# Dealing the third pass's on-chip buffers anew: input tiles from five to four, residual tiles from three to four, result tiles from one to two

## The chip, the cores and the metric

The kernel runs on 1 core of a Trainium2 chip. The metric is the device time of the whole program in microseconds (us). Everything is float32. The engines are named as the profile names them: PE (matrix multiply; PEld is its weight load), DVE (vector), ACT (scalar), POOL (GpSimd) and SP (SyncE, which issues most of the loads).

## What is computed

The input x has 8 images of 96 x 96 pixels with 192 channels. Two residual blocks are applied; this case lies in the first one, cut here to what matters:

```python
x = x + L0(gn(x))          # gn: group norm, 32 groups per image
x = x + L1(gn(x))          # L1: 7x7 depthwise conv, layer norm, two-layer MLP
# L0:
proj   = einsum('bhwd,dc->bhwc', x, W_in) + b_in             # 192 -> 384 channels
local  = depthwise_conv_3x3(proj)
mixed  = 0.25 * (lr + rl + tb + bt) + local                  # four moving averages of local
normed = (mixed - mean) * rsqrt(var + 1e-5) * ln_g + ln_b    # over the 384 channels
return einsum('bhwc,cd->bhwd', normed, W_out) + b_out        # 384 -> 192 channels
```

## The kernel before

The program is five passes one after the other, with the intermediate tensors in device memory: A (lines 210 to 331: group norm and the projection, written to `P_d`), B (338 to 436: convolution and moving averages, written to `M_d`), C (446 to 607: layer norm, the output projection and the residual, written to `X1_d`), D (613 to 698: depthwise convolution, written to `Y_d`) and E (706 to 968: layer norm, MLP, residual, output). The change lies in pass C, "the third pass".

Pass C handles 192 units, numbered U = 0 to 191 here. A unit is two columns (WB = 2) of a pair of images (the four pixel columns j, b = 0..1). For each unit:

- `load_c` (486 to 503) issues, all on SP's queue, three loads of `mt` (line 492, 192 KB each, one for each 128 of the 384 channels of `M_d`) and one load of `xr` (line 499, 288 KB, the residual pixels of x).
- `stats_c` (505 to 513): PE transposes `mt` into `pt` (line 508, three instructions for each pixel column), and DVE takes its statistics (`st`, `mv`, lines 512 and 513). After four of these, `rsqrt_eps` makes the scale `rs`: an addition on DVE (`rs_ve`, line 27), then a power on POOL (line 28).
- `out_c` (515 to 525): PE multiplies `mt` with the folded weights into `po` (line 518), and ACT scales `po` by `rs` into `xo` (line 525).
- POOL adds a constant row to `xr` in place (line 568), and adds `xo` and `xr` into `x1c` (line 591).

These three POOL steps are called X_U (line 568), r_U (line 28) and A_U (line 591) from here on. 24 units fill one `x1c` tile, half of an image pair. After A_23, A_47, ... the tile is stored by four stores of 1728 KB on POOL's own queue (line 597), and the next 24 units are interleaved with the group statistics of the stored tile on DVE (`gn_st`, line 538, 64 steps). After the second half of a pair (A_47, A_95, A_143, A_191) these end in `group_scale` with one long power on POOL (`gn_sh`, line 28). The seven places between two `x1c` tiles inside the pass are called the boundaries: four "odd" ones (after units 23, 71, 119, 167) and three "even" ones (after 47, 95, 143).

What sets the order: the tile library allots each tile name a ring of `bufs` buffers. The n-th tile of a ring with k buffers waits until the last reader of tile n - k is done. The library's scheduler fixes each engine's order of instructions when the program is built; it isn't the order of the source. Each engine, and SP's queue, then works in that fixed order, and an instruction whose operands aren't ready holds up all behind it. In steady work the built order of before is, on each queue (m_U is one of the three loads of `mt`, x_U the load of `xr`, p_U transposes, o_U products):

```
POOL  X_U  r_(U-1)  A_(U-2)      then  X_(U+1)  r_U  A_(U-1)  ...
SP    m_(U+2) m_(U+2)  x_U  m_(U+2)   then the same for U+1 ...
PE    p_U o_(U-1)  four times, alternating, then p_(U+1) o_U ...
```

PSUM rings in pass C: three buffers for `pt`, four for `po`. `x1c` has two buffers, the small tiles `rs`, `mv`, `st` two each.

Of the kernel before, what the change touches and what calls it, by code (L numbers as in the profile page):

```python
# [8 lines left out]
F32 = mybir.dt.float32  # L9
# [13 lines left out]
def rsqrt_eps(nc, pool, out, var, eps, neg_half, tag):  # L23

    rows, n = out.shape
    t = pool.tile([rows, n], F32, tag=tag, name=tag)
    nc.vector.tensor_scalar(t, var, eps, None, ALU.add)  # L27
    nc.gpsimd.tensor_tensor(out, t, neg_half[:rows, :n], ALU.pow)  # L28
# [60 lines left out]
def conv_blocks_kernel(  # L89
# [32 lines left out]
    B, S, _, D = x.shape  # L122
# [3 lines left out]
    NC = C // 128  # L126
# [211 lines left out]
    with ExitStack() as ph:  # L338
        cp = ph.enter_context(tc.tile_pool(name="b_const", bufs=1))
        ip = ph.enter_context(tc.tile_pool(name="b_in", bufs=2))  # L340
# [98 lines left out]
    WB = 2  # L439
# [6 lines left out]
    with ExitStack() as ph:  # L446
        cp = ph.enter_context(tc.tile_pool(name="c_const", bufs=1))
        xp = ph.enter_context(tc.tile_pool(name="c_x", bufs=2))
        ip = ph.enter_context(tc.tile_pool(name="c_in", bufs=2))
# [36 lines left out]
        def load_c(u):  # L486

            bp, _, w = place(u)
            b = slice(2 * bp, 2 * bp + 2)
            mt = ip.tile([128, NC, WB, 2, S], F32, tag="mt", name="mt", bufs=5)  # L490
            for m in range(NC):
                nc.sync.dma_start(
                    mt[:, m].rearrange("c w b h -> c w (b h)"),
                    M_d[S - w - WB : S - w, m * 128 : (m + 1) * 128, b, :].rearrange(
                        "w c b h -> c w (b h)"
                    ),
                )
            xr = ip.tile([S, 2, WB, D], F32, tag="xr", name="xr", bufs=3)
            nc.sync.dma_start(
                xr.rearrange("h b w c -> h b (w c)"),  # L500
                x[b, :, w : w + WB, :].rearrange("b h w c -> h b (w c)"),
            )
            return mt, xr

        def stats_c(mt, mv, j, b):
            pt = ps_t.tile([128, C], F32, tag="pt", name="pt")
            for m in range(NC):
                nc.tensor.transpose(  # L508
                    pt[:S, m * 128 : (m + 1) * 128], mt[:, m, WB - 1 - j, b, :], ident
                )  # L510
            st = sp.tile([S, 6], F32, tag="st", name="st")
            nc.vector.bn_stats(st, pt[:S])  # L512
            nc.vector.bn_aggr(mv[:, 2 * j + b, :], st)

        def out_c(mt, rs, xo, j, b):
            po = ps_o.tile([128, D], F32, tag="po", name="po")
            for m in range(NC):
                nc.tensor.matmul(  # L518
                    po[:S],
                    mt[:, m, WB - 1 - j, b, :],  # L520
                    wc[:, m],
                    start=(m == 0),
                    stop=(m == NC - 1),
                )
            nc.scalar.mul(xo[:, b, j, :], po[:S], rs[:, 2 * j + b : 2 * j + b + 1])  # L525

        def group_steps(x1c, bp, part):

            if part == 0:
                gn[0] = sp.tile([S, 2 * GROUPS, NH, 6], F32, tag="gn_st", name="gn_st", bufs=1)  # L530
                gn[1] = sp.tile([S, 2 * GROUPS, 2], F32, tag="gn_mv", name="gn_mv", bufs=1)
            st, mv = gn
            xf = x1c.rearrange("p c w b -> p (c w) b")
            n = GS * WC

            def step(b, g):
                k = b * GROUPS + g
                nc.vector.bn_stats(st[:, k, part], xf[:, g * n : (g + 1) * n, b])  # L538
                if part == NH - 1:
                    nc.vector.bn_aggr(mv[:, k], st[:, k].rearrange("p a b -> p (a b)"))  # L540

            def last():
                sh = group_scale(nc, sp, ps_s, mv, avg, neg_half)
                nc.vector.tensor_copy(
                    s1[:, :, :, bp], sh.rearrange("p a (b g) -> p a b g", b=2)
                )

            steps = [lambda b=b, g=g: step(b, g) for g in range(GROUPS) for b in range(2)]
            return steps + [last] if part == NH - 1 else steps
# [5 lines left out]
        def place(u):  # L555
            k, w = divmod(u, n_c)
            return k // NH, k % NH, (k % NH) * WC + w * WB

        ahead = [load_c(0), load_c(1)]
        held = None  # L560
        x1c = None
        steps = []
        for u in range(n_u + 1):
            if u < n_u:
                mt, xr = ahead.pop(0)
                if u + 2 < n_u:
                    ahead.append(load_c(u + 2))
                nc.gpsimd.tensor_tensor(  # L568
                    xr.rearrange("p b w c -> p (b w) c"),
                    xr.rearrange("p b w c -> p (b w) c"),  # L570
                    cst.unsqueeze(1).to_broadcast([S, 2 * WB, D]),
                    ALU.add,
                )
                mv = sp.tile([S, 2 * WB, 2], F32, tag="mv", name="mv")
            if held is not None:
                mt_h, rs_h, xr_h = held
                bp_h, part_h, w_h = place(u - 1)
                w_h -= part_h * WC
                if w_h == 0:
                    x1c = xp.tile([S, D, WC, 2], F32, tag="x1c", name="x1c")  # L580
                xo = ip.tile([S, 2, WB, D], F32, tag="xo", name="xo", bufs=1)
            for j in range(WB):
                for b in range(2):
                    if u < n_u:
                        stats_c(mt, mv, j, b)
                    if held is not None:
                        out_c(mt_h, rs_h, xo, j, b)
                    if steps and u % n_c >= 2:
                        steps.pop(0)()
            if held is not None:  # L590
                nc.gpsimd.tensor_tensor(  # L591
                    x1c[:, :, w_h : w_h + WB].rearrange("p c w b -> p b w c"), xo, xr_h, ALU.add
                )
                if w_h + WB == WC:
                    for q in range(4):
                        c = slice(q * D // 4, (q + 1) * D // 4)
                        nc.gpsimd.dma_start(
                            X1_d[:, c, bp_h, part_h * WC : (part_h + 1) * WC], x1c[:, c]
                        )
                    steps = group_steps(x1c, bp_h, part_h)  # L600
            held = None
            if u < n_u:
                rs = sp.tile([S, 2 * WB], F32, tag="rs", name="rs")
                rsqrt_eps(nc, sp, rs, mv[:, :, 1], LN0_EPS, neg_half, "rs_ve")
                held = (mt, rs, xr)
# [7 lines left out]
    with ExitStack() as ph:  # L613
        cp = ph.enter_context(tc.tile_pool(name="d_const", bufs=1))
        ip = ph.enter_context(tc.tile_pool(name="d_in", bufs=2))
# [93 lines left out]
    with ExitStack() as ph:  # L709
        cp = ph.enter_context(tc.tile_pool(name="e_const", bufs=1))  # L710
        ip = ph.enter_context(tc.tile_pool(name="e_in", bufs=2))
# [203 lines left out]
        for u in range(n_u + 1):  # L915
            cur, nxt = u < n_u, u + 1 < n_u
            if cur:
# [3 lines left out]
                xo = tp.tile([S, 2, WH, D], F32, tag="xo", name="xo")  # L921
# [94 lines left out]
```

## Time and profile before

| | us |
|---|---|
| median of 3 runs | 8308.31 (8305.22 to 8310.41) |
| the profiled execution, its own time | 8301.38 |
| its span in the profile | 8299.2 |
| pass C in the trace: first X step to the end of A_191 | 3036.8 to 4746.9 |
| A_U to A_(U+1) in the steady stretches, median | 8.1 |
| granted PE clock over the span | 0.964 |

The profile's page lists busy time by engine, the chain of work that ended last (followed back from the last instruction through what released each step), and groups of instructions with busy time, mean duration and the idle time of the engine ahead of them. "x192" is a count, `a<-b,c` is output from inputs by tile name. The trace also answers for a window: the chain in order of time, or each engine's instructions with the idle time ahead of them in brackets and what ended it.

Of the stretch that pass C takes, these rows of idle time stand out on the page: ACT waits 1206.2 us ahead of line 525 (`xo`) for line 591, POOL waits 572.5 us ahead of line 568 for the load of `xr`, and PE waits 332.5 us ahead of line 518 for line 525.

### The profile page before, as it was taken

What the parts mean: (1) busy time and instruction counts of PE and PEld (TensorE: products, weight loads), DVE (VectorE), ACT (ScalarE), POOL (GpSimd) and SP (SyncE); (2) the same over time, 40 slices, a digit from 0 to 9 for tenths busy, and PEclk for the clock granted to TensorE, in tenths of its full rate; (3) what the DMA queues carried; (4) which work ended last, traced back from release to release, by engine and by line L of the source; (5) the groups of instructions that cost most, each with busy time, mean ns of one, the idle gap of its engine ahead of it and who ended that gap; (6) DMA issues with size and microseconds to landing.
All of it is one profiled execution on the core that took longest, in us unless ns stands there. A gap on an engine that the chain in (4) does not pass through costs nothing.

```text
span 8299.2 us, 102681 instructions
## 1 busy us (share of the span) xinstructions
PE 7574.8 (91%) x39318; PEld 4652.6 (56%) x39318; DVE 4808.9 (58%) x10307; ACT 2146.4 (26%) x4322; POOL 2196.9 (26%) x1586
## 2 busy tenths in 40 slices
PE   6999999999999986676667689998999999999999
PEld 4666554444444456565666567775555555555555
DVE  4555399999999974444444444444444444444442
ACT  2333311111111111111111145552222222222222
POOL 1111133333333345555555511111000000000000
PEclk9999999999999998888888899999999999999999
DMA  9995355555555544444444487775444444443332
GB/s 213 239 238 194 131 136 135 134 137 136 136 140 136 136 112 137 125 137 124 135 135 117 125 206 197 196 186 100 67 69 69 66 69 69 66 68 63 61 57 38
DMA packets 1322605, 1044.64 MB, mean 126 GB/s; under 512 B 1051383, under 2 KB 1237960, under 8 KB 1301384
## 3 DMA queue, kind: packets, MB, share of 16 engines
q1 hardware_dynamic: 1247272, 641.39, 37.9%
q0 software_dynamic: 74240, 396.39, 15.3%
q8 instruction: 315, 5.16, 0.3%
q14 instruction: 170, 1.39, 0.1%
q10 hardware_dynamic: 608, 0.30, 0.0%
HBM read 639.70 MB, written 431.30 MB: 129 GB/s over the span
## 4 chain that ended last, share of the span: by engine, by line
PE 55%; issue 12%; POOL 12%; DMA 9%; DVE 2%; ACT 0%; SPq 0%; POOLq 0%; DVEq 0%
PE pl L381 17%; PE hp L857 8%; PE po L883 8%; DMA xr<-in_x_dram 7%; PE pa L404 6%; PE hp L867 5%; PE po L897 4%; POOL x1c L591 4%; POOL xr L568 4%; POOL rs L28 2%; PE pt L816 2%; PE pt L828 2%; POOL Y_d L694 1%; PE pm L283 1%; DVE gn_st L538 1%
## 5 line engine op out<-in xcount | busy, mean ns | idle before, releaser
L381 PE MATMUL pl<-pin,band 96*96 96x380 f32 (+1 forms) x4608 | 1541.1, 484 | 13.7 <-issue 13.7
L518 PE MATMUL po<-wc,mt 128*96 128x192 f32 x4608 | 978.7, 356 | 332.9 <-ACT xo L525 332.5
L381 PEld LDWEIGHTS pl<-pin,band 96*96 96x96 f32 x4608 | 752.1, 163 | 742.9 <-issue 621.0
L394 DVE TENSOR_TENSOR_SCAN fw<-decay,loc 96x768 f32<-96x768 f32 x384 | 1049.4, 2733 | 15.4 <-ACT loc L389 15.4
L400 POOL TENSOR_TENSOR both<-fw,bw 96x768 f32<-96x768 f32 x384 | 694.3, 1808 | 1283.7 <-DVE bw L396 1283.7
L518 PEld LDWEIGHTS po<-wc,mt 128*96 128x96 f32 x4608 | 783.8, 180 | 392.9 <-ACT xo L525 373.7
L668 PE MATMUL py<-xn,band 64*48 64x372 f32 (+3 forms) x10752 | 855.1, 477 | 21.6 <-DVE xn L640 21.6
L512 DVE BATCH_NORM_STATS2 st<-pt 96x6 f32<-96x384 f32 x768 | 430.0, 564 | 765.0 <-PE pt L508 764.5
L28 POOL TENSOR_TENSOR rs<-rs_ve,neg_half 96x4 f32<-96x4 f32 (+1 forms) x288 | 354.1, 1229 | 1887.2 <-DVE rs_ve L27 1886.9
L857 PE MATMUL hp<-yT,w0w 128*128 128x384 f32 x2304 | 798.7, 490 | 0.1
L283 PE MATMUL pm<-xT,win 96*128 96x384 f32 x2304 | 798.7, 497 | 0.0
L820 DVE COPY yT<-pt 128x384 f32<-128x384 f32 x288 | 160.6, 558 | 1098.6 <-PE pt L816 1098.6
L883 PE MATMUL po<-g,w1g 128*128 128x384 f32 x2304 | 792.9, 487 | 0.0
L389 ACT COPY loc<-pl 96x384 f32<-96x384 f32 x768 | 364.8, 475 | 1649.6 <-PE pl L381 1547.4
L876 ACT ACTIVATE g<-hp,b0g 128x384 f32<-128x384 f32 x1152 | 575.1, 581 | 811.3 <-PE hp L867 811.3
L668 PEld LDWEIGHTS py<-xn,band 64*48 64x48 f32 x10752 | 606.4, 120 | 269.8 <-issue 23.7
L396 DVE TENSOR_TENSOR_SCAN bw<-decay,loc 96x768 f32<-96x768 f32 x384 | 662.0, 1724 | 0.0
L640 DVE TENSOR_SCALAR xn<-xin,s 128x96 f32<-128x96 f32 x1536 | 375.6, 343 | 462.1 <-PE py L668 451.9
L525 ACT ACTIVATE xo<-po,rs 96x192 f32<-96x192 f32 x768 | 262.0, 413 | 1464.3 <-POOL x1c L591 1206.2
L404 PE MATMUL pa<-loc,mix 96*96 96x384 f32 x1536 | 575.9, 498 | 4.3 <-DVE mo L414 4.3
L283 PEld LDWEIGHTS pm<-xT,win 96*128 96x128 f32 x2304 | 431.3, 194 | 261.9 <-issue 16.2
L508 PE MATMUL pt<-ident,mt 128*96 128x128 f32 x2304 | 418.4, 296 | 165.7 <-DMA mt<-M_d 125.2
(96 smaller groups left out, 8196.5 us busy)
## 6 DMA issues: line engine op xcount, KB each, us to landing
P_d<-po POOLq DMA_DIRECT2D x96, 1152.0 KB, 6.5
pin<-P_d SPq DMA_DIRECT2D x96, 1152.0 KB, 9.3
M_d<-mo POOLq DMA_DIRECT2D x96, 1152.0 KB, 5.9
mt<-M_d SPq DMA_DIRECT2D x576, 192.0 KB, 3.6
xin<-X_d SPq DMA_DIRECT2D x96, 768.0 KB, 9.0
ximg<-in_x_dram SPq DMA_DIRECT2D x32, 1728.0 KB, 25.0
xr<-in_x_dram SPq DMA_DIRECT2D x192, 288.0 KB, 3.4
X_d<-x1c POOLq DMA_DIRECT2D x32, 1728.0 KB, 24.8
```

What stands on the lines that cost most here:

```text
L28: nc.gpsimd.tensor_tensor(out, t, neg_half[:rows, :n], ALU.pow)
L283: nc.tensor.matmul(pm, win[:, k, m * 128 : (m + 1) * 128], xT[:, k], start=(k == 0), stop=(k == 1),)
L381: nc.tensor.matmul(pls[g][:S, :, lo:hi], band[:, c, kh, :], pin[:, c, g * GB : (g + 1) * GB, lo + kh - 1 : hi + kh - 1], start=(n == 0), s ...
L394: nc.vector.tensor_tensor_scan(fw, decay_f, loc, 0.0, ALU.mult, ALU.add)
L396: nc.vector.tensor_tensor_scan(bw[:, ::-1], decay_f, loc[:, ::-1], 0.0, ALU.mult, ALU.add)
L400: nc.gpsimd.tensor_tensor(both, fw, bw, ALU.add)
L404: nc.tensor.matmul(pa[:S], mix, loc[:, g * GB * S : (g + 1) * GB * S], start=True, stop=True)
L518: nc.tensor.matmul(po[:S], mt[:, m, WB - 1 - j, b, :], wc[:, m], start=(m == 0), stop=(m == NC - 1),)
L668: nc.tensor.matmul(pys[g][q * 64 : q * 64 + HS, :, lo:hi], band[rows, c, kw, :], xn[rows, c, q * BQ : (q + 1) * BQ, lo + 2 * (kw - 3) : hi ...
L857: nc.tensor.matmul(hps[m, q], w0w[:, 2 * q, m * 128 : (m + 1) * 128], yT[:, 2 * q], start=True, stop=False,)
L876: nc.scalar.activation(g[:, m, q], hps[m, q], AF.Gelu, bias=b0g[:, m : m + 1], scale=1.0)
L883: nc.tensor.matmul(po, w1g[:, m, :128], g[:, m, q], start=(m == 0), stop=(m == NE - 1))
```

## The change

Three ring sizes in pass C change; no instruction is added, taken out or rewritten.

```diff
-            mt = ip.tile([128, NC, WB, 2, S], F32, tag="mt", name="mt", bufs=5)
+            mt = ip.tile([128, NC, WB, 2, S], F32, tag="mt", name="mt", bufs=4)
...
-            xr = ip.tile([S, 2, WB, D], F32, tag="xr", name="xr", bufs=3)
+            xr = ip.tile([S, 2, WB, D], F32, tag="xr", name="xr", bufs=4)
...
-                xo = ip.tile([S, 2, WB, D], F32, tag="xo", name="xo", bufs=1)
+                xo = ip.tile([S, 2, WB, D], F32, tag="xo", name="xo", bufs=2)
```

A partition holds 4608 bytes of `mt`, 3072 of `xr` and 3072 of `xo`, so the three rings together grow from 35,328 to 36,864 bytes per partition. What lies behind them moves up by 1536 bytes. One consequence: the preparation tiles of pass C (`wo`, `gb`, `bo`, `mean_w`, `lnb`; lines 459 to 484) no longer share bytes with pass A's `po`, so the scheduler puts their four loads and the `mean_w` and `lnb` steps at the very start of the program; before, they stood at the start of pass B.

The scheduler also deals the queues of pass C anew. In steady work the built order is now:

```
POOL  X_(U+1)  r_(U-1)  A_(U-2)  then  X_(U+2)  r_U  A_(U-1)  ...
SP    m_U m_U m_U  x_U           then the same for U+1 ...
PE    as before
```

At a boundary the order of before and of after is (shown for the first odd one; D is a store of `x1c`):

```
before POOL  D D D D A24 | r25 X26 r26 A25 | r27 X27 X28 A26 | r28 X29 A27 | r29 A28 | X30 X31 r30 A29
after  POOL  D D D D A24 | r25 r26 X27 A25 | r27 X28 X29 A26 | r28 A27 | r29 X30 A28 | X31 X32 r30 A29
before SP    x26 m28 m29 m29 m29 m30 m30 m30 x27 x28 m31 m31 x29
after  SP    x27 m28 m28 m28 m29 m29 m29 x28 x29 m30 m30 m30 x30
before PE    p27 p28 p29 (12 each), 3 of p30, o26 o27 o28 (12 each), then alternating
after  PE    p27 p28 p29 (12 each), o26 o27 o28 (12 each), then p30 and o29 alternating
DVE, both    statistics of p27, p28 and half of p29, then 43 gn_st steps, then the rs_ve of r27, ...
```

The even boundaries differ in this: all statistics steps that are left (49) and the `group_scale` chain stand behind the first half of p53's statistics, and POOL's long `gn_sh` step stands ahead of A49. At the end of the pass, POOL's order is `X191 r190 A189 | r191 A190 | A191` before and `X191 r189 A188 | r190 A189 | r191 A190 | A191` after. At the start it is `X0 X1 X2 r0 A0` before and `X0 X1 X2 X3 r0 A0` after. The order of instructions in passes D and E is the same.

## The prediction

> **What bounds the kernel now.** I read the groups first, then the chain of work in a steady stretch of pass C, then a boundary, queue by queue. The groups with their idle time and all that ended it (busy, mean ns of one, idle before and releasers):
>
> ```profile
> L568 POOL TENSOR_TENSOR xr<-xr,cst 96x768 f32<-96x768 f32 x192 | 346.2, 1804 | 577.8 <-DMA xr<-in_x_dram 572.5 <-DVE cst L484 5.0
> ...
> L525 ACT ACTIVATE xo<-po,rs 96x192 f32<-96x192 f32 x768 | 262.0, 413 | 1464.3 <-POOL x1c L591 1206.2 <-POOL rs L28 163.8 <-PE po L518 94.0
> ```
>
> ACT waits 1206 us for A steps, because `xo` has one buffer; POOL waits 572 us for loads of `xr`. Which of the two sets the end is seen in the chain in order of time (start, us, what):
>
> ```profile
> 4001.82 3.30 DMA xr<-in_x_dram
> ...
> 4005.25 1.80 POOL xr L568
> 4007.05 0.98 POOL rs L28
> 4008.03 1.82 POOL x1c L591
> ...
> 4009.86 3.35 DMA xr<-in_x_dram
> ```
>
> One turn is load of `xr` 3.3, X 1.8, r 1.0, A 1.8, with 0.2 of small steps: 8.1 us a unit. ACT isn't in it, so the 1206 us lie off the path. The A step at 4008.03 frees the buffer that the load at 4009.86 fills. By the built order that load is for X_(U+2), and POOL has put X_(U+2) ahead of A_U. So the load, two units ahead of its use, is still waited for in every turn.
>
> The boundary after A_23 (ends 3233.06) is the other place. First SP's queue in order of time (start, duration, count at the end):
>
> ```profile
> 3233.46 13.41 SPq L492 DMA_DIRECT2D mt<-M_d  x7
> ```
>
> Then PE, with its idle time in brackets:
>
> ```profile
> 3250.77 2.37 PE L508 MATMUL pt<-ident,mt 128*96 128x128 f32 x10 [2.79 <-DMA mt<-M_d]
> 3258.76 0.42 PE L508 MATMUL pt<-ident,mt 128*96 128x128 f32 x1 [5.63 <-DMA mt<-M_d]
> 3265.60 0.45 PE L508 MATMUL pt<-ident,mt 128*96 128x128 f32 x1 [6.42 <-DMA mt<-M_d]
> 3270.13 0.45 PE L508 MATMUL pt<-ident,mt 128*96 128x128 f32 x1 [4.08 <-DMA mt<-M_d]
> ```
>
> And POOL:
>
> ```profile
> 3268.08 1.01 POOL L28 TENSOR_TENSOR rs<-rs_ve,neg_half 96x4 f32<-96x4 f32 x1 [9.03 <-DVE rs_ve L27]
> 3273.31 1.80 POOL L568 TENSOR_TENSOR xr<-xr,cst 96x768 f32<-96x768 f32 x1 [4.21 <-DMA xr<-in_x_dram]
> 3276.49 1.80 POOL L568 TENSOR_TENSOR xr<-xr,cst 96x768 f32<-96x768 f32 x1 [1.38 <-DMA xr<-in_x_dram]
> ```
>
> Seven loads of `mt` go out beside the four 1728 KB stores of `x1c`; the fourth lands at 3250.7 and lets p29 go on, the fifth to seventh (unit 30) at 3258.6, 3265.5 and about 3270.1, against 3.6 us in quiet. POOL's r_27 waits for DVE, which has run 43 `gn_st` steps after the first statistics of p29.
>
> **What the Trainium skill says.** "DMA: Bandwidth & Descriptors", section "Queues, rings and completion order": descriptors of one ring are consumed in ring order, and each DMA engine goes round the rings that have work, packet by packet. The trace agrees: after A_23 the loads land in the order of issue, 3.8, 5.5, 11.5, 17.7, 25.6, 32.5 and 37.1 us after its end, some 6 us apart beside the stores. "Perfetto Trace Analysis", section "Optimization Strategy": the same gap repeating on an engine can mean that there isn't memory for the next tile. The trace shows such a gap (3.4 us ahead of each X), but the order of POOL decides whether a further buffer closes it. Section "Sequencer Loop" there: an engine's instruction waits for its semaphores; here the trace shows the rest of the stream waiting behind it, as r_27 did for 9.03 us.
>
> **Part 1, `xr` from three to four.** The scheduler hoists X by the same one unit: after, X_(U+3) stands ahead of A_U, and its buffer is that of unit U - 1, freed by A_(U-1). So the turn stays A_(U-1), load 3.3, X 1.8, r 1.0, A_U 1.8. Steady cost: nothing, 8.1 us a unit. The loads beside it are the same (three of `mt` right behind each `xr`), and m_(U+4), which now stands ahead of x_(U+4) on SP, waits for o_U, which ran a turn earlier. If SP were late there, each 0.1 us would cost some 15 us over the 150 steady units.
>
> **Part 2, `xo` from one to two.** ACT may start on r_U instead of on the end of the last A, 1.8 us earlier in the turn. Nothing waits for it in the steady turn (A_U comes a whole turn after r_U), so nothing is gained there. It helps only at the tail, below.
>
> **Part 3, `mt` from five to four.** In steady work it costs nothing: m_(U+4) needs o_U done and is issued more than a turn ahead of p_(U+4). At a boundary it does cost. m29 now takes the buffer of m25 and must wait for o25. PE ends o25 at 3241.4 (p26 and o25 were held by DVE statistics that stand behind `gn_st` steps, which wait for A_23; that stays). SP issued m30 of before at 3241.55 on just that wait. So after A_23 the queue carries three loads of m28, then from 3241.5 three of m29: m29's last is the sixth behind the stores, where it was the fourth. Before, the fourth and sixth landed at these us after the A step (b is the unit):
>
> b 23: 17.7, 32.5; 47: 17.7, 30.6; 71: 15.8, 28.7; 95: 16.3, 31.6; 119: 17.6, 33.0; 143: 15.9, 29.4; 167: 16.0, 29.7.
>
> The shift is 14.8, 12.9, 12.9, 15.3, 15.4, 13.5, 13.7: 98.5 us in all, 14.1 a boundary. Behind p29 wait, in DVE's order, 43 `gn_st` steps and the `rs_ve` of r_27; behind that, all of POOL.
>
> Odd boundary, worked for b = 23 with POOL's steps at A 1.8, X 1.8, r 1.0: m29 is there at 3265.55; first statistics done 1.35 later, 43 steps 15.4 (3252.45 to 3267.85 before), so r_27 runs 3282.5 to 3283.5. X28, X29 (loads landed by 3276.4) to 3287.1, A26 3288.9, r28, A27 3291.7, r29 3292.7, X30 3294.5, A28 3296.3, X31 3298.1, X32 waits for its load (issued at 3296.3, plus 3.4) and ends at 3301.6, r30 3302.6, A29 3304.4. Before, A_29 ended at 3299.05. So of 14.8 us 9.4 are taken back, since X27 no longer waits for a load (4.2 us) and fewer X stand in the way; 5.4 remain. In general A_29 ends 38.85 us after the sixth landing. Against the ends of before (66.0, 62.4, 66.2, 62.5 after the A step) the four odd ones cost 5.4 + 5.2 + 5.7 + 6.1 = 22.4 us.
>
> Even boundary, b = 47: `gn_sh` started 25.5 us after the fourth landing, and everything between is DVE's and PE's chain; it ends at 3512.0 instead of 3499.1. From its end to A_53 before took 27.3 us. After: A49 1.8, r 1.0, X52 1.8, X53 (load 3.4 after A49, then 1.8), A50 1.8, r 1.0, A51 1.8, r 1.0, X54 1.8, A52 1.8, X55 1.8, X56 (load 3.4 after A52, then 1.8), r 1.0, A53 1.8: 24.3 us. So 3.0 are taken back, 3.1 and 3.3 at the other two: 9.9 + 12.2 + 10.2 = 32.3 us.
>
> **Part 4, the ends.** Tail: from the end of A_187 (4722.75) to A_191 (4746.9) took 24.2 us, with two loads on the path (4722.8, 4730.5) and `xo` in turn. After, one load is left, and xo_190 follows r_190; A_191 ends some 17.5 us after A_187: 6.7 less (between 4 less, if PE runs o_191 at half pace as it did, and 7). Start of pass C: X3 ahead of r_0 delays it by 0.8, of which ACT's wait hides some: 0.5 more. Start of program: `lnb` on DVE (1.36 us) and the wait for `gb` come ahead of the second filter write, on which the first image's load waits. `gb` took 6.0 us to land in pass B, a quiet small load 1.9: 1.7 to 4.6 more, I take 2.5; the 1.5 us of `lnb` and `mean_w` leave pass B, where DVE is full: 1.0 more. Passes D and E have the same order: nothing.
>
> **Sum.** 22.4 + 32.3 - 6.7 + 0.5 + 1.0 = +49.5 us. Against the profiled execution's 8301.4 (2.2 over its span; 0.08% under the median) that is 8351; on the median 8308.3 it is 8358, my forecast, 0.6% slower.
>
> The unknown is where m29's last load lands. If the ring drains one fewer load no sooner, it takes the seventh place (37.1, 35.2, 34.3, 36.0, 37.7, 34.0, 34.0): 32.8 more, 8391. Below, the bound is the fourth place, the rival next.
>
> **Rivals.** *Faster, landing early.* If m29 landed where it did, the odd boundaries would gain 3.5 each and the even 3.1, the ends 5.2: 28.5 less, 8280. For it: one fewer load in the queue, PE and ACT 1.8 us earlier. Against: the wait of m29 for o25, and o25's for DVE. The sum is zero at a mean shift of 7.0 us (98.5 - 49.5 over seven); I expect 14.1. *Faster, the turn opens.* If X ran early enough for the load to leave the turn, POOL's own 4.6 us and PE's 5.2 us a unit would be left: 2.9 us by 150 units, some 435 less, 7873. Against it stands the built order of POOL. *No change:* shift near 7 us, 8308. *Slower by more:* the seventh place, 8391.
>
> **Chances.** Forecast (sixth place, give or take 3 us a boundary) 0.62; seventh place or beyond 0.20; no change 0.10; landing early 0.06; turn opens 0.02. I call 0.2%, 16.6 us, what a measurement can tell from no change. Faster 0.08, same 0.11 (with a little from the low edge of the forecast), slower 0.81. The range is 8322 to 8395: it takes in the sixth and seventh places and leaves out the gains.
>
> **What would show it.** Steady A to A stays 8.1 us with load, X, r, A in the chain; ACT's 1206 us ahead of `xo` mostly vanish at no gain. At each boundary PE waits for `mt` in p29 until about 30 us after the A step instead of 17, DVE's `gn_st` steps stand behind it, r_27 or `gn_sh` starts about 14 us later, and A_29 or A_53 ends 5 or 11 us later. I am wrong if the steady turn isn't 8.1, if p29 goes on before 24 us, or if passes A, B, D or E change by more than 5 us.

## The result, and the profile after

| | before | after |
|---|---|---|
| median, us (runs of both on the same chip) | 8306.76 (8301.94 to 8310.41) | 8390.61 (8389.39 to 8392.6) |
| span of the profiled execution | 8299.2 | 8389.0 |
| granted PE clock over the span | 0.964 | 0.958 |
| pass C: end of A_0 to end of A_191 | 1699.4 | 1784.8 |
| A to A, median of the steady stretches | 8.1 | 8.1 |

The change makes the kernel slower: ratio 1.0102, 95% interval 1.0084 to 1.0119. That is 84 us where the forecast said 50; it lies in the range, at the time given for the rival "seventh place" (8391). The two profiled executions, from which the rest of this section is read, lie 89.5 us apart.

The groups of the kernel after (busy, mean ns of one, idle before and what ended it):

```profile
L568 POOL TENSOR_TENSOR xr<-xr,cst 96x768 f32<-96x768 f32 x192 | 345.5, 1801 | 543.6 <-DMA xr<-in_x_dram 538.5 <-DVE cst L484 5.0
...
L525 ACT ACTIVATE xo<-po,rs 96x192 f32<-96x192 f32 x768 | 262.1, 412 | 1550.4 <-POOL rs L28 1323.3 <-PE po L518 227.0
```

ACT no longer waits for an A step (1206 us before, now none), and waits as long for r steps instead. POOL still waits 538 us for loads of `xr` (572 before): the fourth buffer took nothing out of the turn, as the chain in a steady stretch shows (start, us, what):

```profile
4058.72 1.80 POOL xr L568
4060.52 0.98 POOL rs L28
4061.49 1.81 POOL x1c L591
...
4063.32 3.30 DMA xr<-in_x_dram
...
4066.75 1.80 POOL xr L568
```

It is the same turn as before, load 3.3, X 1.8, r 1.0, A 1.8. The time was lost at the boundaries. After A_23 (which ends at 3238.02) SP's queue carries six loads of `mt` instead of seven (start, duration, count at the end):

```profile
3238.48 13.87 SPq L492 DMA_DIRECT2D mt<-M_d  x6
```

Then PE in p29, with its waits in brackets:

```profile
3263.90 0.42 PE L508 MATMUL pt<-ident,mt 128*96 128x128 f32 x1 [11.46 <-DMA mt<-M_d]
3271.12 0.45 PE L508 MATMUL pt<-ident,mt 128*96 128x128 f32 x1 [6.80 <-DMA mt<-M_d]
3274.84 2.37 PE L508 MATMUL pt<-ident,mt 128*96 128x128 f32 x10 [3.27 <-DMA mt<-M_d]
```

Before, p29 waited once and went on 17.7 us after the A step. Now it waits for each of m29's three loads and goes on after 36.8 us. POOL pays for it:

```profile
3292.15 1.01 POOL L28 TENSOR_TENSOR rs<-rs_ve,neg_half 96x4 f32<-96x4 f32 x1 [29.34 <-DVE rs_ve L27]
3293.14 3.56 POOL L568 TENSOR_TENSOR xr<-xr,cst 96x768 f32<-96x768 f32 x2
3296.66 1.82 POOL L591 TENSOR_TENSOR x1c<-xo,xr 96x768 f32<-96x768 f32 x1
3298.44 1.01 POOL L28 TENSOR_TENSOR rs<-rs_ve,neg_half 96x4 f32<-96x4 f32 x1
3299.43 1.83 POOL L591 TENSOR_TENSOR x1c<-xo,xr 96x768 f32<-96x768 f32 x1
```

r_27 starts 54.1 us after A_23 (35.0 before). From there POOL works without a wait, X28, X29, A26, r28, A27, so some of the loss is taken back. The table gives all seven boundaries, in us after the A step: the landing of m29's last load (and of the like load elsewhere), and the end of the sixth A step after it.

| after A of unit | 23 | 47 | 71 | 95 | 119 | 143 | 167 |
|---|---|---|---|---|---|---|---|
| landing, before | 17.7 | 17.7 | 15.8 | 16.3 | 17.6 | 15.9 | 16.0 |
| landing, after | 36.8 | 36.2 | 32.9 | 35.9 | 35.2 | 30.4 | 35.7 |
| sixth A, before | 66.0 | 81.1 | 62.4 | 80.1 | 66.2 | 79.6 | 62.5 |
| sixth A, after | 76.5 | 96.6 | 72.6 | 97.6 | 74.2 | 91.3 | 74.8 |

The landings shift by 126.1 us in all, the ends by 85.7. A_0 ends 3.6 later, the tail (A_187 to A_191) is 6.4 shorter, and the other 145 units take 6.1 more. That makes the 89.0 by which A_191 ends later; passes D and E add 0.8.

### The profile page after: what moved, and what is told of

Same layout as the page of the kernel before. It is cut to its first block, busy times and chain, and to the rows that moved or that the text cites. A ratio compares the mean times of both kernels' runs of the same rounds, so it can differ in the third digit from the quotient of the medians.

```text
span 8389.0 us, 102672 instructions
## 1 busy us (share of the span) xinstructions
PE 7581.7 (90%) x39318; PEld 4668.6 (56%) x39318; DVE 4878.7 (58%) x10307; ACT 2142.8 (26%) x4322; POOL 2195.6 (26%) x1586
## 4 chain that ended last, share of the span: by engine, by line
PE 61%; POOL 11%; DMA 9%; issue 5%; DVE 2%; SPq 0%; POOLq 0%; ACT 0%; DVEq 0%
PE pl L381 17%; PE hp L857 8%; PE po L883 8%; PE py L668 7%; DMA xr<-in_x_dram 6%; PE pa L404 6%; PE hp L867 5%; PE po L897 4%; POOL x1c L591 4%; POOL xr L568 4%; POOL rs L28 2%; DMA mt<-M_d 2%; PE pt L816 2%; PE pt L828 2%; DVE gn_st L538 1%
## 5 line engine op out<-in xcount | busy, mean ns | idle before, releaser
L668 PEld LDWEIGHTS py<-xn,band 64*48 64x48 f32 x10752 | 610.6, 120 | 265.7 <-issue 24.1
## 6 DMA issues: line engine op xcount, KB each, us to landing
X_d<-x1c POOLq DMA_DIRECT2D x32, 1728.0 KB, 24.1
```

The lines of the kernel that those rows point to most:

```text
L668: nc.tensor.matmul(pys[g][q * 64 : q * 64 + HS, :, lo:hi], band[rows, c, kw, :], xn[rows, c, q * BQ : (q + 1) * BQ, lo + 2 * (kw - 3) : hi ...
```

## The experiments

The theory: `mt` with four buffers makes m29 late, that is the whole loss, and `xr` and `xo` move nothing in steady work. The rivals: the new order of the X steps costs; the waits that vanished were on the path; a load's place in the queue, or else its time of issue, sets its landing.

**1. Undoing the `mt` part.**

```diff
-            mt = ip.tile([128, NC, WB, 2, S], F32, tag="mt", name="mt", bufs=4)
+            mt = ip.tile([128, NC, WB, 2, S], F32, tag="mt", name="mt", bufs=5)
```

> The kernel after with `mt` given back its fifth buffer; `xr` 4 and `xo` 2 stay. Theory (the whole loss comes from m29, whose loads must wait for o25 and so go out beside the stores): the last load of m29 lands some 16 to 18 us after the A step as before, steady turn 8.1 us, the boundaries end 3 us earlier than before, the tail is some 6 us shorter, and the time is 8275 to 8290. Rival (the loss comes from the new order of the X steps on POOL and of the four loads at the start of the program): the boundaries stay as late as in the kernel after, 8350 to 8390.

Measured: 8297.96 us, before beside it 8301.47; ratio 0.9995 (0.9986 to 1.0003). The loss is gone, m29's last load lands 13.5 to 18.7 us after the A step, and the tail is 4.7 us shorter. But the time is 8 us above the range that I expected, since the 3 us at each boundary aren't there: their sixth A steps end 2.9 us earlier in all seven together. POOL at the first boundary of this kernel shows one reason (X29, A26, r28, X30, A27):

```profile
3273.06 1.81 POOL L568 TENSOR_TENSOR xr<-xr,cst 96x768 f32<-96x768 f32 x1 [1.39 <-DMA xr<-in_x_dram]
3274.82 1.83 POOL L591 TENSOR_TENSOR x1c<-xo,xr 96x768 f32<-96x768 f32 x1
3276.60 1.02 POOL L28 TENSOR_TENSOR rs<-rs_ve,neg_half 96x4 f32<-96x4 f32 x1
3280.05 1.81 POOL L568 TENSOR_TENSOR xr<-xr,cst 96x768 f32<-96x768 f32 x1 [2.42 <-DMA xr<-in_x_dram]
3281.81 1.83 POOL L591 TENSOR_TENSOR x1c<-xo,xr 96x768 f32<-96x768 f32 x1
```

With five `mt` buffers the scheduler puts X30 ahead of A27, and X30 waits for a load that A26 has just let go. With four, X30 stands behind A27 and the wait isn't there. So what the fourth `xr` buffer gives at a boundary depends on the order that the scheduler builds, and that changes with the number of `mt` buffers.

**2. The `mt` part alone**, on the kernel before.

```diff
-            mt = ip.tile([128, NC, WB, 2, S], F32, tag="mt", name="mt", bufs=5)
+            mt = ip.tile([128, NC, WB, 2, S], F32, tag="mt", name="mt", bufs=4)
```

> The kernel before with only `mt` from 5 to 4. Theory (m29 late): the last load of m29 lands 30 to 37 us after the A step; nothing of `xr` or `xo` takes any of it back, so the loss is larger than in the kernel after: seven shifts of 18 to 20 us are 131, less what the loads of x27 and x28 gain, 8400 to 8440. Rival (order of the X steps and the start): 8305 to 8325.

Measured: 8413.06 us, ratio 1.0128 (1.0114 to 1.0142), within the theory's 8400 to 8440. The boundaries end 113.3 us later than before, and m29's loads wait in the same way (PE in p29):

```profile
3261.98 0.42 PE L508 MATMUL pt<-ident,mt 128*96 128x128 f32 x1 [9.13 <-DMA mt<-M_d]
3266.19 0.45 PE L508 MATMUL pt<-ident,mt 128*96 128x128 f32 x1 [3.78 <-DMA mt<-M_d]
3272.06 2.37 PE L508 MATMUL pt<-ident,mt 128*96 128x128 f32 x10 [5.42 <-DMA mt<-M_d]
```

Here POOL's order at the first boundary is that of before, and no load of pass C stands at the start of the program. So the order of the X steps and those loads are out as the cause. The changes of `xr` and `xo` take back 28 of 113 us at the boundaries, but only beside the damage.

**3 and 4. `xr` alone, `xo` alone**, on the kernel before.

```diff
-            xr = ip.tile([S, 2, WB, D], F32, tag="xr", name="xr", bufs=3)
+            xr = ip.tile([S, 2, WB, D], F32, tag="xr", name="xr", bufs=4)
```

> The kernel before with only `xr` from 3 to 4. Theory: the steady turn stays 8.1 us, because the scheduler moves X by the same one unit; the boundaries take back about 3 us each since X27 no longer waits for a load, the tail a few us: 8275 to 8295. Rival (the turn opens with a fourth buffer): steady turn below 6 us, about 7900. Rival (order of the X steps costs): above 8325.

```diff
-                xo = ip.tile([S, 2, WB, D], F32, tag="xo", name="xo", bufs=1)
+                xo = ip.tile([S, 2, WB, D], F32, tag="xo", name="xo", bufs=2)
```

> The kernel before with only `xo` from 1 to 2. Theory: ACT is off the path, its 1206 us of waiting for line 591 vanish and the time does not: 8295 to 8307. Rival (those 1206 us were on the path): several hundred us less.

Measured: 8295.92, ratio 0.9993 (0.9985 to 1.0001), and 8299.49, ratio 0.9995 (0.9987 to 1.0003). Each interval holds 1; the first time is 1 us above the range that I expected. The steady turn is 8.1 us in both. With `xo` at two, ACT's 1206 us of waiting for A steps are gone from its group and the time stands:

```profile
L525 ACT ACTIVATE xo<-po,rs 96x192 f32<-96x192 f32 x768 | 263.7, 413 | 1455.7 <-POOL rs L28 1284.1 <-PE po L518 171.6
```

**5. Place in the queue or time of issue?** In the kernel after, m28's loads (and those of the like unit elsewhere) are issued on ACT's queue.

```diff
-                nc.sync.dma_start(
+                (nc.scalar if u % n_c == 4 else nc.sync).dma_start(
                     mt[:, m].rearrange("c w b h -> c w (b h)"),
```

> The kernel after, with the three loads of m28 (and of the same unit at each other boundary) issued on ACT's queue instead of SP's, so that m29's loads are the first to third that SP's queue holds behind the stores; nothing else moves. Theory of the prediction (the place in the queue sets the landing): m29's last load lands 16 to 20 us after the A step, 8300 to 8330. Rival (a load's time of issue, some 9 to 12 us after the A step, sets it, because all share the same engines with the stores): it lands at 30 to 37 us as in the kernel after, 8385 to 8395.

Measured: 8390.49 us against 8390.61 of the kernel after; ratio to before 1.0108 (1.0093 to 1.0123). After A_23 (3240.20) SP's queue now holds one load of `xr` and, as its only loads of `mt`, m29's three. First that queue, then PE in p29:

```profile
3240.23 0.34 SPq L499 DMA_DIRECT2D xr<-in_x_dram  x1
3249.71 5.22 SPq L492 DMA_DIRECT2D mt<-M_d  x3
```

```profile
3263.86 0.42 PE L508 MATMUL pt<-ident,mt 128*96 128x128 f32 x1 [9.23 <-DMA mt<-M_d]
3269.27 0.45 PE L508 MATMUL pt<-ident,mt 128*96 128x128 f32 x1 [4.99 <-DMA mt<-M_d]
3275.71 2.37 PE L508 MATMUL pt<-ident,mt 128*96 128x128 f32 x10 [6.00 <-DMA mt<-M_d]
```

Issued at 3249.7, 3250.1 and 3253.0, they land 23.5, 29.0 and 35.5 us after the A step, as late as in the kernel after. A table over the kernels, each number a mean of the seven boundaries, in us after the A step, puts it together:

| load of `mt` | place among the `mt` loads on SP's queue | issued | landed |
|---|---|---|---|
| before, m29's last | fourth | 1.9 | 16.7 |
| before, m30's last | seventh | 10.9 | 35.5 |
| after, m29's last | sixth | 11.6 | 34.7 |
| `mt` alone, m29's last | seventh | 11.3 | 35.8 |
| m28 on ACT's queue, m29's last | third | 12.0 | 35.3 |

Place third, sixth or seventh: some 35 us, if issued at 11 to 12. The rival's expectation held: the place is out.

The Trainium skill ("DMA: Bandwidth & Descriptors", section "Queues, rings and completion order") has each DMA engine go round the rings that have work, packet by packet. The packets in the trace of the kernel after agree: from 3254 to 3262 us, 498 of the stores (1.99 MB) and 499 of SP's loads (0.37 MB) went through. But turn for turn isn't byte for byte: a packet of the stores has mostly 4224 bytes, one of `mt` 768, so the loads get a sixth of the bytes in that stretch. Before that, from 3248 to 3252, there were 259 packets of the stores and none of the loads, though the first of m29's was issued at 3247.35. Why the loads stand at first, and why the last of them lands only about when the third store does (34.7 and 34.3 us after the A step, mean of the seven boundaries), the runs don't tell.

**6. The stores two units apart.** In the source of the kernel after, one store of `x1c` now follows A_23, the next A_25, and so on. The scheduler puts each but the first somewhat earlier; after A_23 they start 0.3, 5.8, 26.1 and 54.5 us after its end.

```diff
-                    for q in range(4):
-                        c = slice(q * D // 4, (q + 1) * D // 4)
-                        nc.gpsimd.dma_start(
-                            X1_d[:, c, bp_h, part_h * WC : (part_h + 1) * WC], x1c[:, c]
-                        )
+                    def store(q, x1c=x1c, bp_h=bp_h, part_h=part_h):
+                        c = slice(q * D // 4, (q + 1) * D // 4)
+                        nc.gpsimd.dma_start(
+                            X1_d[:, c, bp_h, part_h * WC : (part_h + 1) * WC], x1c[:, c]
+                        )
+
+                    stores = [(u + 2 * q, q, store) for q in range(4)]
...
+            while stores and (stores[0][0] <= u or u == n_u):
+                _, q, store = stores.pop(0)
+                store(q)
```

> The kernel after, with the four stores of an `x1c` tile issued one by one, two units apart, instead of together after its last A step. Theory (the stores delay m29's loads and so the boundary): m29's loads land within 10 us of issue, PE waits for `mt` in p29 no later than 20 us after the A step, and the boundaries lose a third to a half of what they cost over steady work: 8250 to 8340. Rival (the 43 group statistics that stand ahead of `rs_ve` on DVE are what the boundary costs, and the loads lie beside them): 8370 to 8395.

Measured: 8257.13 us, ratio to before 0.9948 (0.9932 to 0.9965), 133 us under the kernel after. PE at the first boundary (A_23 ends at 3237.80):

```profile
3259.88 0.42 PE L508 MATMUL pt<-ident,mt 128*96 128x128 f32 x1 [7.01 <-DMA mt<-M_d]
3260.91 0.93 PE L508 MATMUL pt<-ident,mt 128*96 128x128 f32 x2 [0.61 <-DMA mt<-M_d]
```

m29's last load, issued at 11.4 as in the kernels above, lands 23.2 us after the A step on the mean instead of 34.7. So the stores are what delays it. It takes not the 10 us from its issue that I had expected at most, but 12: the first two stores are still on their way when it is issued. It lands within 1.0 us of the second of them at every boundary; in the three kernels with four `mt` buffers above it lands within 2.4 us of the third. The gain isn't the landing's alone, though. The orders of PE and POOL changed too (here POOL; A24's wait is gone):

```profile
3238.10 1.85 POOL L598 DMA_DIRECT2D X_d<-x1c  x1 [0.30 <-POOL x1c L592]
3239.97 1.84 POOL L592 TENSOR_TENSOR x1c<-xo,xr 96x768 f32<-96x768 f32 x1
```

A24 ends 4 us after A_23, where four stores in a row keep it to some 19. The boundary also lasts longer here, until the tenth unit; the first ten units after the boundaries take 682 us in all, 130 less than in the kernel after (812), which is nearly the whole gain. How it divides between the landing and the new orders isn't settled.

**7 and 8. Taking the load out of the turn.** The constant row is added to `xo` just ahead of the A step, not to `xr` on arrival. The sum and the number of POOL steps stay; the step can't run ahead of ACT's `xo`, so no POOL step waits for a fresh load. First with the buffers of after (4, 4, 2), then with `mt` at five.

```diff
-                nc.gpsimd.tensor_tensor(
-                    xr.rearrange("p b w c -> p (b w) c"),
-                    xr.rearrange("p b w c -> p (b w) c"),
-                    cst.unsqueeze(1).to_broadcast([S, 2 * WB, D]),
-                    ALU.add,
-                )
...
             if held is not None:
+                nc.gpsimd.tensor_tensor(
+                    xo.rearrange("p b w c -> p (b w) c"),
+                    xo.rearrange("p b w c -> p (b w) c"),
+                    cst.unsqueeze(1).to_broadcast([S, 2 * WB, D]),
+                    ALU.add,
+                )
```

> The kernel after, with the constant row added to `xo` just ahead of the A step instead of to `xr` on arrival (same sum, same count of POOL steps), so that no POOL step waits for a fresh load of `xr`. Theory (the steady turn is A, load 3.3, X, r, A, and the fourth `xr` buffer did not open it because X ran ahead by the same one unit): the turn falls from 8.1 us to what PE (5.2) or POOL (4.6) needs, 5.2 to 6.0 us; by 150 units 300 to 440 us less than the kernel after, 7940 to 8080. Rival (the turn is held by something else, bandwidth or PE's waits): steady turn above 7.5 us, above 8300.

> The same with `mt` at five buffers. Theory: turn as in the run with four; at the boundaries m29 is issued beside or ahead of the stores and the seven boundaries end earlier by 60 to 110 us in all: 7840 to 7990, and faster than the run with four. Rival (with the turn open, m29's wait for o25 costs nothing): within 20 us of the run with four.

Measured: 7938.25 (ratio to before 0.9564, 0.9550 to 0.9579) and 7824.79 (0.9429, 0.9415 to 0.9443), the latter the fastest of all. They lie 2 and 15 us below the ranges that I expected. The steady turn is 5.2 us, and the chain in it is PE alone (the run with four `mt` buffers):

```profile
4000.32 0.33 PE pt L508 x3
4000.65 0.97 PE po L518 x6
4001.62 0.33 PE pt L508 x3
4001.95 0.97 PE po L518 x6
```

Four times 0.33 and 0.97 are the 5.2 us. The group of the moved step shows the 538 us of waiting for loads gone:

```profile
L585 POOL TENSOR_TENSOR xo<-xo,cst 96x768 f32<-96x768 f32 x192 | 346.6, 1805 | 1.5 <-ACT xo L525 1.5
```

The fifth `mt` buffer is worth 113 us here: the first eight units after a boundary take 636 us in all with four, 518 with five; the steady units take 581 and 580.

**9 and 10. Which buffers matter once the turn is open.** The same edit on the kernel before (5, 3, 1), and with `xo` at two (5, 3, 2).

> The kernel before (five, three, one buffers) with the constant row added to `xo` just ahead of the A step. Theory: with the load out of the turn, the single `xo` buffer comes on the path: from the end of A to the next A there lie four ACT steps of 0.41 us and two POOL steps of 1.8 us, 5.3 us and some 0.3 between them, so the turn is 5.3 to 5.8 us and the time 7830 to 7920. Rival (one `xo` buffer is still covered by PE's 5.2 us): 7820 to 7830, as with five, four and two.

> The same with `xo` at two buffers and `xr` still at three. Theory (the fourth `xr` buffer is worth nothing in either form): within 8 us of five, four and two, 7817 to 7833. Rival (with a turn of 5.2 us the load of `xr` needs the fourth buffer): above 7850.

Measured: 7888.34 (0.9497, 0.9482 to 0.9511) and 7830.46 (0.9426, 0.9412 to 0.9440). The fourth `xr` buffer is worth nothing that can be told from noise here either. The second `xo` buffer is now worth 58 us. With one, ACT is held by every A step (first ACT, then POOL, in the units after a boundary):

```profile
4051.92 1.34 ACT L525 ACTIVATE xo<-po,rs 96x192 f32<-96x192 f32 x4 [4.75 <-POOL x1c L591]
4058.00 1.34 ACT L525 ACTIVATE xo<-po,rs 96x192 f32<-96x192 f32 x4 [4.74 <-POOL x1c L591]
```

```profile
4053.40 1.80 POOL L585 TENSOR_TENSOR xo<-xo,cst 96x768 f32<-96x768 f32 x1 [1.51 <-ACT xo L525]
4055.16 1.01 POOL L28 TENSOR_TENSOR rs<-rs_ve,neg_half 96x4 f32<-96x4 f32 x1
4056.15 1.82 POOL L591 TENSOR_TENSOR x1c<-xo,xr 96x768 f32<-96x768 f32 x1
4059.49 1.80 POOL L585 TENSOR_TENSOR xo<-xo,cst 96x768 f32<-96x768 f32 x1 [1.52 <-ACT xo L525]
```

The turn is 6.1 us in these units, where PE has run ahead, against 4.5 in the same units with two buffers; in the steady stretch, where PE needs its 5.2, it is 5.26 against 5.21, a little under the 5.3 that I had expected at least.

**11 and 12. Both edits**, stores apart and the row added to `xo`, with four and with five `mt` buffers.

> The kernel after with both edits: constant row added to `xo`, and the four stores two units apart. Theory (m29's loads beside the stores are what four `mt` buffers cost): the boundaries fall from 71 and 94 us (for six units) to 50 to 75, and most of the 113 us that lie between four and five `mt` buffers are gone: 7760 to 7860. Rival (the fifth buffer is worth 113 us for another reason): 7900 to 7940.

> As the run before with `mt` at five buffers, the candidate for the fastest. Theory: the fifth buffer is now worth little, within 30 us of the run with four, 7740 to 7830. Rival: over 60 us faster than with four.

Measured: 7908.32 (0.9520, 0.9504 to 0.9536) and 7893.73 (0.9504, 0.9489 to 0.9518). With four buffers, spreading the stores gains 30 us; with five it costs 69. One expectation held: with the stores apart the fifth `mt` buffer is worth 15 us instead of 113. The times missed: both lie above their ranges, the first in that of its rival. So these two runs don't show that the fifth buffer's worth is its cover against the stores. With five buffers m29's last load still lands earlier (10.5 us after the A step, 23.0 with four), yet the sixth A steps end no earlier (547 us over the seven boundaries in both), so something else holds the boundary. The scheduler deals PE's work there in longer blocks, and POOL waits for products (five buffers, first boundary):

```profile
3230.90 1.80 POOL L586 TENSOR_TENSOR xo<-xo,cst 96x768 f32<-96x768 f32 x1 [13.06 <-ACT xo L525]
...
3243.15 1.80 POOL L586 TENSOR_TENSOR xo<-xo,cst 96x768 f32<-96x768 f32 x1 [7.69 <-ACT xo L525]
```

In the first of these waits PE itself stands 10.2 us for m32's loads: the first is issued at 3212.0, 2.4 us after the fourth store starts, and lands at 3223.1, 0.5 us after that store. I didn't try the spread stores with PE's order held as it was.

## Why the prediction was right, and which term was too small

**Part 1, `xr`: right.** The turn stays 8.1 us with the load in it; experiment 3 shows that the fourth buffer alone does nothing that can be measured, 7 and 8 that the turn opens when the step no longer waits for the load. The size that I gave that rival (7873) was about right: the edit that opens the turn gave 7825 with five `mt` buffers.

**Part 2, `xo`: right.** ACT's 1206 us lay beside other work (experiment 4). They come onto the path when the turn is 5 us (experiment 9).

**Part 3, `mt`: right in the chain of waits, a third too small (54.7 us at the boundaries, 85.7 measured).** m29 waits for o25, lands late behind the stores, DVE and then POOL stand behind it. The term that failed is the landing: I put it at the "sixth place", 98.5 us of shift; the measured shift is 126.1. Its rule was wrong, not only its size. I had read the landings of before by their place in the queue and gave m29 the sixth. But m29's last load is issued 11.6 us after the A step, when before's seventh load was issued (10.9), not its sixth (8.9 after A_23), and it lands like it. I had even the right time of issue, that of m30 of before, and then counted places from it. My text gave the other reading as "if the ring drains one fewer load no sooner", with 0.20 for it; experiments 2 and 5 show that its landing was the one to take, though not for its place.

**What is taken back: right.** At the odd boundaries the sixth A ends 39.0 to 39.7 us after the landing (38.85 in the text), at the even ones 24.1 us after `gn_sh` at the first (24.3). In sum 40 us are taken back of 126, where I had 44 of 98. But the rival "landing early" was mispriced: it took a gain of 3.5 us at each odd and 3.1 at each even boundary, 23.3 in all, and experiment 1, which lands early, has 2.9.

**Part 4, the ends: right within a few us.** The tail is 6.4 shorter (6.7 in the text), the start of pass C itself 0.8 longer (0.5). The first image's load comes 0.7 us later. Pass C begins 2.8 later (1.0 in the text), but over the kernels with X on `xr` its first X step lies between 3034.8 and 3041.6, early and late ones both with the four loads at the start of the program and without, so I can't lay the rest to the change.

**The sum with the measured landings:** 126.1 - 40.4 + 3.6 - 6.4, and 6.1 in the other units, which I had at nothing, give the 89.0 by which A_191 ends later. That the median falls on the 8391 of the "seventh place" is in part chance: that sum has 87.5 us at the boundaries where 85.7 were measured, it lacks the 6.1 and most of the later start, and the medians lie some 6 us closer together than the profiled executions.

## What to carry to other kernels

Read a transfer's delay beside a burst of stores from another transfer that was issued at the same time after the burst began, not from one with the same place in the queue. A buffer can be worth what it lets start ahead of the burst: with four stores in a row the fifth `mt` buffer was worth 113 us. What it is worth with the stores apart isn't shown, since another wait held the boundary there. Where a wait for a load survives another buffer, look at which step waits for it: moving one addition from the loaded tile to the computed one took 8.1 us a unit to 5.2, where a buffer more had done nothing.

## What the runs showed of the hardware that was not expected

A load of 192 KB that lands in 3.6 us in quiet (median of the kernel before) takes 13 to 25 us when it is issued 8 to 12 us after an A step that is followed by four stores of 1728 KB on POOL's queue (kernel after, m29's loads), and 14 to 23 when m28's loads are in another queue (A_23 of experiment 5). Beside the stores its packets of 768 bytes take turns with theirs of 4224.

The four store instructions hold POOL longer than their own 1.8 us each. In the kernel after, the fourth stands 9.87 us, and the profile names nothing that it waits for:

```profile
3238.32 5.48 POOL L597 DMA_DIRECT2D X_d<-x1c  x3 [0.30 <-POOL x1c L591]
3253.67 1.79 POOL L597 DMA_DIRECT2D X_d<-x1c  x1 [9.87 <-issue]
```

The landings show it: the first store lands at 3253.26, and the fourth starts 0.42 us later. In the eleven kernels that issue four in a row, 88 bursts in all, the fourth starts 0.31 to 0.42 us after the first has landed. So no more than three of these stores were on their way at a time. For this the next A step of the kernel after ends 17.4 to 20.5 us after the last. With the stores two units apart (experiment 6) each took 1.8 us at the seven boundaries, and none stood.
